# One of seven block products by 128-output matmuls, key sums and key rows by 32-output ones, and batch 2's rows loaded later, in a graph attention kernel

## The chip, the core and the metric

The kernel runs on one core of one Trainium2 chip. The metric is device time in microseconds (us) of one execution, as the median of several. A core has five engines that work side by side: TensorE (PE; its weight loads are shown as PEld), VectorE (DVE), ScalarE (ACT), GpSimd (POOL) and SyncE (SP), whose queue issues most DMAs here. TensorE multiplies a stationary operand (the loaded weights) with a moving one that streams by. All data is fp32.

## The reference

For each of 16 batches there are 512 rows `v` of 512 features, one conditioning row `q`, and an adjacency of 512 x 512 x 11 integers. Two attention directions attend from all 512 rows to the first 20 rows, with 16 heads of 32 features:

```python
row_zero = v.sum(-1) == 0
vcq = concatenate([v, where(row_zero[..., None], 0.0, q[:, None, :])], axis=-1)
self_feat = vcq @ W_self.T + b_self
output = self_feat
for d in range(2):
    A = adj if d == 0 else swapaxes(adj, 1, 2)
    A = A[:, :, :20, :]
    kv = self_feat[:, :20]
    aff = einsum(self_feat @ Wq[d].T + bq[d], kv @ Wk[d].T + bk[d]) / sqrt(32)
    aff = where(A.sum(-1) > 0, aff, -9e15) + A @ w_bias + b_bias
    w = softmax(aff)                       # over the 20 rows, for each head
    output += einsum(einsum(w, kv), Wout[d]) + bout[d]
return v + relu(output)
```

## The kernel before

**Setup (about the first 92 us).** Weights are loaded, and what depends on the first 20 rows of all batches at once (320 columns) is computed. The key sums (`kv_terms`, L532, tiles `ps_kv`) multiply 128 x 128 blocks of `W_self` with those rows: 16 matmuls with 128 outputs. The key rows (`key_rows`, L581, tiles `ps_k`) multiply `Wk`: eight calls of four 128-output matmuls, four calls ahead of the first burst of `keys` and one ahead of each of the next four bursts (L669, 32-row matmuls into `ps_g`). The `keys` bursts fold `Wq` and the keys into one matrix per batch, which goes to DRAM (`g_d`). Values (L644, `ps_v`) and batch 0's own features (`self_feat`, L202, `ps_sf`) lie between the bursts, in an order written out in `plan`. The row flags of batches 0 and 1 (L186, `ps_nz`) come from matmuls.

**The loop over 16 batches, four row tiles `nt` each.** All instructions are in a hand-written order (`manual_schedule`); each engine works through its own list in that order, SP's DMA queue too. While batch b is in its softmax stages, the features of batch b + 1 are made by a seven-product block scheme (`product`, L279; the sums of row blocks in `x_sum`, L244; sums joined in `partial` and `joined`): products 1 and 2 at `nt == 2`, products 6, 7 and 5 at `nt == 3`, products 4 and 3 at `nt == 0` of the next batch. Each product is two output halves times two input halves times four matmuls with 32 outputs and 246 columns, each four writing to the four 32-partition strips of one PSUM tile. Product 2 has a PSUM tile of its own, `ps_d`; the others share `ps_a` and `ps_c`.

Per row tile, `scores` (L353) makes 64 matmuls with 32 outputs and 152 columns into one of two `ps_s` tiles; `weigh` (DVE), `expo` (ACT), `normal` (DVE and POOL) and `turn` (DVE) make the softmax and its transpose. At `nt == 2` `attend` (L426, `ps_o`) applies the weights of the batch before to its values, with 32-row matmuls; `finish` and `residual` complete the output. At the very end the identity matmuls of `put_self` (L774) have 128 outputs.

A row whose sum is zero gets no `q`. For batches 2 and up, `load_xn` loads the batch's rows (two DMAs of 512 KB), `row_sum` (L166, four ACT instructions) sums them, `row_mask` (L170) turns the sums into flags on POOL and stores them by SP, and `load_nz` spreads them to all partitions for `partial`. For batch 2 the rows are loaded at batch 0, `nt == 1`, behind `load_adj(1, 1)`; their sums are made at batch 0, `nt == 3`, and the flags early in batch 1, `nt == 0`. `blocks` (L159) copies the values into block form by twelve DMAs at batch 0, `nt == 2`, after `clear_blocks` (L142) has filled the target with zeros; `load_values` (L136) reads it.

Of the kernel before, what the change touches and what calls it, by code (L numbers as in the profile page):

```python
# [13 lines left out]
P = 128  # L14
# [4 lines left out]
def gat_kernel(  # L19
# [20 lines left out]
    nc = tc.nc  # L40
    B, F, N = xT.shape
    NG, L = adj.shape[3], adj.shape[4]
    H, DH = 16, 32
    C = F // P
    HL = P // DH
    NT = N // P
    BM = B * NG
# [4 lines left out]
    R = P // HL  # L52
# [54 lines left out]
    def load_xn(b, h, ins=None):  # L107
        t = xns[b, h] = load.tile([P, 2, F], F32, tag="xn", name=f"xn{b}_{h}")
        behind(nc.sync.dma_start(t, xn[b].rearrange("(p j) f -> p j f", j=4)[:, 2 * h : 2 * h + 2]), ins)

    def load_adj(b, h, ins=None):
        t = adjs[b, h] = load.tile([P, 2, S * L], I32, tag="adj", name=f"adj{b}_{h}", bufs=3)
        a = adj[b, h * 2 * P : (h + 1) * 2 * P].rearrange("(t p) d m l -> p t (d m l)", p=P)
        behind(nc.sync.dma_start(t, a), ins)
# [131 lines left out]
    def product(b, n):  # L246

        w, x = {
            1: ((0, 0), lambda: x_block(b, 0, 0)),
            2: ((0, 1), lambda: x_block(b, 1, 0)),  # L250
            3: (3, lambda: x_block(b, 1, 1)),
            4: ((1, 1), lambda: sums[b, 4]),
            5: (0, lambda: sums[b, 1]),
            6: (1, lambda: sums[b, 2]),
            7: (2, lambda: sums[b, 3]),
        }[n]
        x = x()
        if n == 1:
            parts[b, "a"] = [bank(f"ps_a{b}_{i}", i) for i in range(2)]
        if n == 2:  # L260
            parts[b, "d"] = bank(f"ps_d{b}", 2)
        if n == 5:
            parts[b, "c"] = bank(f"ps_c{b}", 3)
        for i in range(2):
            for k in range(2):
                for a in range(HL):
                    at = i * P + a * R
                    if isinstance(w, tuple):
                        lhs = ws_v[:, 2 * w[1] + k, bass.ds(w[0] * F // 2 + at, R)]
                    else:  # L270
                        lhs = ws_s[:, w, k, bass.ds(at, R)]
                    if n in (2, 3, 5):
                        to = parts[b, "d" if n == 2 else "c"][bass.ts(a, R), bass.ts(i, HN)]
                        start = k == 0 if n == 2 else (n, i, k) == (5, 0, 0)
                        stop = k == 1 if n == 2 else (n, i, k) == (3, 1, 1)
                    else:
                        to = parts[b, "a"][i][bass.ts(a, R), :HN]
                        start, stop = (n, k) == (1, 0), (n, k) == (4, 1)
                    nc.tensor.matmul(to, lhs, x[:, k], start=start, stop=stop, skip_group_check=n != 2)  # L279
# [56 lines left out]
    def full_add(b, nt):  # L336
        f = fulls[b, nt] = msk.tile([P, H * S], F32, tag="full", name=f"full{b}_{nt}").rearrange(
            "p (g h m) -> p g h m", g=HL, m=S
        )
        shape = [P, HL, HL, S]  # L340
        nc.gpsimd.tensor_add(  # L341
            f, cqs[b].unsqueeze(1).to_broadcast(shape),
            adds[b, nt // 2][:, nt % 2].unsqueeze(2).to_broadcast(shape),
        )
# [108 lines left out]
    with tc.tile_pool(name="setup", bufs=1) as sp, tc.tile_pool(name="ps_acc", bufs=4, space=PSUM) as acc["pool"]:  # L453
# [18 lines left out]
        with tc.tile_pool(name="setup_k", bufs=1) as sk:  # L472
# [56 lines left out]
            kv_ps = [bank(f"ps_kv{fc}") for fc in range(C)]  # L529

            def kv_terms(fc, k):
                nc.tensor.matmul(  # L532
                    kv_ps[fc][:, :BM], ws_v[:, k, bass.ts(fc, P)], xkv[:, k],
                    start=(k == 0), stop=(k == C - 1),
                )

            for k in range(2):
                for fc in range(C):
# [38 lines left out]
            def key_rows(d, jc):  # L577

                ps = bank(f"ps_k{d}{jc}")
                for k in range(C):  # L580
                    nc.tensor.matmul(  # L581
                        ps[:, :BM], wk_sb[d][:, k, bass.ts(jc, P)], kvT[:, k],
                        start=(k == 0), stop=(k == C - 1),
                    )
                p3 = ps[:, :BM].rearrange("p (b m) -> p b m", m=NG)
                kh0 = msk.tile([P, B], F32, tag="kh0", name=f"kh0{d}{jc}", bufs=4)
                nc.scalar.activation(kh0, p3[:, :, 0], AF.Identity, bias=bk_sb[:, d, jc : jc + 1])
                nc.vector.scalar_tensor_tensor(
                    khD[:, d * C + jc].rearrange("p (b m) -> p b m", m=ND), p3[:, :, 1:],
                    bk_sb[:, d, jc : jc + 1], kh0.unsqueeze(2).to_broadcast([P, B, ND]),  # L590
                    ALU.add, ALU.subtract,
                )
# [176 lines left out]
    with tc.manual_schedule():  # L769
# [11 lines left out]
        for b in range(B):  # L781
# [7 lines left out]
            for nt in range(NT):  # L789
# [3 lines left out]
                if b == 0 and nt == 1:  # L793
                    load_adj(1, 0)
                    load_cq(1)
                    clear_blocks(zero)
                    load_adj(1, 1)
                    load_xn(2, 0)
                    load_xn(2, 1)
                if b == 0 and nt == 2:  # L800
                    blocks()
                if nt == 2 and last or nt == 3 and b == 0:
                    load_values(b)

# [7 lines left out]
                if nt == 0:  # L812
                    if b == 0:
                        for g in range(2):
                            scores(b, nt, g, ps[g])
                        mask_sum(b, 1)
                    else:
                        mask_mul(b, 1)
                        product(b, 4)
                        for g in range(2):  # L820
                            scores(b, nt, g, ps[g], range(2))
                        normal(*prev)
                        partial(b, 4, 1, 0, block(b, 1, 0))
                        if more:
                            load_x(b + 1, range(2), done["exp"])
                            load_x(b + 1, range(2, C), done["partial"])
                        for g in range(2):
                            scores(b, nt, g, ps[g], range(2, C))
                        if more:
                            row_mask(b + 1)  # L830
                        mask_count(b, 1)
                        joined(b, 3, "c", 1, 1)
                        product(b, 3)
                        mask_sum(b, 1)
                        if more:
                            load_adj(b + 1, 0, done["masks"])
                    mask_spread(b, 1, (0, 1))
                    if last:
                        biased = work.tile([P, C, N], F32, tag="o", name="biased")
                        for c in (2, 3):  # L840
                            nc.scalar.activation(biased[:, c], sfs[b][:, c], AF.Identity, bias=bo[:, c : c + 1])
                    s = weigh(b, nt, pair)
                    expo(s)
                    mask_spread(b, 1, (2, 3))
                    if prev is not None:
                        turn(*prev)
                    full_add(b, 1)
                    if more:
                        x_sum(b + 1, 1)
                    else:  # L850
                        for c in (2, 3):
                            nc.gpsimd.tensor_add(biased[:, c, N - P :], biased[:, c, N - P :], xs[b][:, c, N - P :])
# [60 lines left out]
                if nt == 3 and more:  # L913
                    mask_count(b + 1, 0)
                    product(b + 1, 6)
                    new_self(b + 1)
                    joined(b + 1, 1, "d", 0, 0)
                    x_sum(b + 1, 4)
                    if b + 2 < B:
                        for j in range(4):  # L920
                            row_sum(b + 2, j)
                    normal(*prev)
                    partial(b + 1, 2, 0, 1)
                    mask_sum(b + 1, 0)
                    if b > 0:
                        load_keys(b + 1, range(2, C), done["masks"])
                    mask_spread(b + 1, 0)
                    for g in range(2):
                        scores(b, nt, g, ps[g])
                    product(b + 1, 7)  # L930
                    product(b + 1, 5)
                    s = weigh(b, nt, pair, lambda: partial(b + 1, 3, 1, 1))
                    expo(s)
                    turn(*prev)
                    if b > 0:
                        residual(b - 1, 2, o)
                        store()
                        load_values(b)
                        residual(b - 1, 3, o)
                    full_add(b + 1, 0)  # L940
# [24 lines left out]
        b = B - 1  # L965
# [80 lines left out]
```

## Time and profile before

| | before |
|---|---|
| time, median of 3 | 592.53 us (591.71 to 592.59) |
| the profiled execution's own time | 593.27 us |
| its span | 591.5 us |
| TensorE busy | 578.7 us, 98% |
| weight loads busy | 439.7 us, 74% |
| VectorE, ScalarE, GpSimd busy | 492.3, 395.6, 384.2 us |
| granted TensorE clock | 0.995 of full |
| moved by DMA | 124.10 MB, 210 GB/s |

The page of the profile gives busy times for each engine. The chain of waits is followed back from the last instruction: its rows are start, duration, engine, output tile and line, and count. The order of time lists instructions by start, with the idle time ahead and what ended it in brackets; "issue" is time in which the engine waited for nothing that the profile shows. An fp32 matmul shows as two records, one per pass, each with a weight load of its own. A form such as `128*32 128x152` is the stationary operand's rows and outputs, and then the moving operand's rows and columns. Matmul ends are modelled, so this document measures from start to start.

### The profile page before, as it was taken

The page shows a single profiled execution, that of the slowest core. Times are in us where ns is not written, and L with a number is a line of the kernel's source. Part 1 is how long each engine was busy: PE and PEld are TensorE (multiplying, and loading weights), DVE is VectorE, ACT ScalarE, POOL GpSimd, SP SyncE. Part 2 cuts the span into 40 slices and gives each one's busy share as a digit, 9 for nine tenths or more (in the row PEclk, how much of TensorE's full clock was granted, in tenths as well). Part 3 has the DMA queues.
Part 4 walks back from the last instruction along what each step waited for, and adds up shares of the span by engine and source line. Part 5 has one row for each costly group of instructions (what it writes and reads, how often), then busy time and mean ns, then how long its engine had stood idle before and what let it go on. Part 6 is the DMA issues. An engine that isn't in the chain of part 4 may idle for free.

```text
span 591.5 us, 30038 instructions
## 1 busy us (share of the span) xinstructions
PE 578.7 (98%) x13180; PEld 439.7 (74%) x13180; DVE 492.3 (83%) x785; ACT 395.6 (67%) x1162; POOL 384.2 (65%) x351
## 2 busy tenths in 40 slices
PE   8999999999999999999999999999999999999994
PEld 6654547888978687787878787788787878787882
DVE  0495565889898888999999999888989898989896
ACT  1234644587877677768686868677787877777661
POOL 2315663638677675758686777675858677776774
PEclk9999999999999999999999999999999999999997
DMA  8998999857848485767676766757585748582503
GB/s 294 385 406 299 332 376 329 257 126 199 223 154 229 155 236 148 206 168 209 184 208 163 223 173 202 171 181 208 164 217 170 216 149 232 158 238 85 167 13 142
DMA packets 98129, 124.10 MB, mean 210 GB/s; under 512 B 19952, under 2 KB 70160, under 8 KB 95952
## 3 DMA queue, kind: packets, MB, share of 16 engines
q1 hardware_dynamic: 96752, 120.31, 67.1%
q8 instruction: 103, 1.69, 1.2%
q0 software_dynamic: 672, 1.36, 1.0%
q10 hardware_dynamic: 576, 0.53, 0.3%
q14 instruction: 26, 0.21, 0.1%
HBM read 82.30 MB, written 40.24 MB: 207 GB/s over the span
## 4 chain that ended last, share of the span: by engine, by line
PE 94%; DVE 3%; DMA 1%; issue 1%; ACT 0%; POOL 0%; SPq 0%; DVEq 0%; POOLq 0%; ACTq 0%
PE ps_s L353 44%; PE ps_a L279 17%; PE ps_c L279 8%; PE ps_o L426 6%; PE ps_d L279 4%; PE ps_v L644 3%; PE ps_k L581 3%; PE ps_sf L202 2%; DMA ws_q<-in_wsT 1%; PE ps_kv L532 1%; DVE o L435 0%; PE ps_nz L186 0%; DVE wt L415 0%; DVE ps_s L371 0%; DVE sm L406 0%
## 5 line engine op out<-in xcount | busy, mean ns | idle before, releaser
L353 PEld LDWEIGHTS ps_s<-g,sf 128*32 128x32 f32 x8192 | 264.0, 110 | 19.8 <-issue 12.2
L353 PE MATMUL ps_s<-g,sf 128*32 128x152 f32 x8192 | 277.3, 293 | 0.5 <-ACT st L684 0.5
L334 ACT COPY both<-add 32x80 f32<-32x80 f32 x512 | 130.9, 256 | 54.8 <-DVE add L325 49.0
L408 POOL TENSOR_TENSOR s<-s,sm 128x640 f32<-128x640 f32 x63 | 80.3, 1275 | 98.0 <-DVE sm L407 98.0
L341 POOL TENSOR_TENSOR full<-cq,both 128x640 f32<-128x640 f32 x64 | 100.1, 1565 | 30.3 <-issue 24.3
L314 ACT ACTIVATE prod<-adj,wb_sb 128x80 f32<-128x80 int32 x330 | 112.5, 432 | 0.0
L380 ACT ACTIVATE s<-s 128x640 f32<-128x640 f32 x63 | 46.5, 738 | 69.4 <-DVE s L375 69.0
L444 POOL TENSOR_TENSOR o<-o,x 128x512 f32<-128x512 f32 x60 | 75.9, 1285 | 0.0
L367 DVE TENSOR_TENSOR full<-ps_s,full 128x608 f32<-128x608 f32 x63 | 49.1, 779 | 32.1 <-PE ps_s L353 26.6
L406 DVE TENSOR_REDUCE sm<-s 128x32 f32<-128x640 f32 x63 | 50.9, 808 | 8.8 <-ACT s L380 8.6
L279 PE MATMUL ps_a<-t,ws_s 128*32 128x246 f32 x960 | 55.5, 370 | 0.0
L371 DVE TENSOR_REDUCE ps_s<-full 128x32 f32<-128x640 f32 x63 | 52.2, 828 | 2.2
L415 DVE STREAM_TRANSPOSE wt<-s 128x640 f32<-128x640 f32 x63 | 52.8, 839 | 0.1
L375 DVE TENSOR_TENSOR s<-full,ps_s 128x640 f32<-128x640 f32 x63 | 51.6, 818 | 1.1
L426 PE MATMUL ps_o<-wt,vd 32*32 32x512 f32 (+5 forms) x816 | 40.8, 581 | 3.7 <-DVE wt L400 2.0
L279 PEld LDWEIGHTS ps_a<-t,ws_s 128*32 128x32 f32 x960 | 32.2, 110 | 15.5
L325 DVE TENSOR_REDUCE add<-prod 128x80 f32<-128x960 f32 x32 | 36.8, 1150 | 6.3 <-ACT prod L314 4.4
L244 POOL TENSOR_TENSOR t<-x 128x492 f32<-128x492 f32 x30 | 34.4, 1148 | 10.1 <-DVE full L367 5.2
L439 ACT ACTIVATE o<-o,bo 128x512 f32<-128x512 f32 x60 | 38.2, 708 | 0.6 <-POOL biased L881 0.6
L435 DVE TENSOR_TENSOR o<-ps_o,sf 128x512 f32<-128x512 f32 x60 | 36.8, 672 | 1.0 <-PE ps_o L426 1.0
L286 DVE SCALAR_TENSOR_TENSOR u<-nz,qw,ps_a 128x246 f32<-128x246 f32 x90 | 36.6, 449 | 0.0
L244 POOL TENSOR_TENSOR t<-x,t 128x492 f32<-128x492 f32 x30 | 34.4, 1147 | 1.2
(238 smaller groups left out, 722.7 us busy)
## 6 DMA issues: line engine op xcount, KB each, us to landing
g_d<-st SPq DMA_DIRECT2D x16, 1064.0 KB, 5.9
g<-g_d SPq DMA_DIRECT2D x28, 608.0 KB, 5.2
out_T<-o SPq DMA_DIRECT2D x60, 256.0 KB, 4.7
xn<-in_xn SPq DMA_DIRECT2D x28, 512.0 KB, 3.6
x<-in_xT SPq DMA_DIRECT2D x28, 512.0 KB, 4.3
adj<-in_adj SPq DMA_DIRECT2D x32, 440.0 KB, 5.0
nz<-nz_d SPq DMA_DIRECT2D x14, 256.0 KB, 4.0
wk<-in_wkT SPq DMA_DIRECT2D x2, 1024.0 KB, 8.0
```

The costliest lines, as they stand in the source:

```text
L244: nc.gpsimd.tensor_sub(t, one, two)
L279: nc.tensor.matmul(to, lhs, x[:, k], start=start, stop=stop, skip_group_check=n != 2)
L314: nc.scalar.activation(p[:, :, l], a[:, :, l], AF.Identity, scale=wb_sb[:, l : l + 1])
L334: nc.scalar.copy(adds[b, h][bass.ts(a, R), :, g], add[r].rearrange("p (t m) -> p t m", t=2))
L341: nc.gpsimd.tensor_add(f, cqs[b].unsqueeze(1).to_broadcast(shape), adds[b, nt // 2][:, nt % 2].unsqueeze(2).to_broadcast(shape),)
L353: nc.tensor.matmul(bank[bass.ts(a, R), bass.ts(j, WD // HL)], sfs[b][:, k, bass.ds(nt * P + (2 * g + j) * R, R)], keys[:, k, a], start=(k ...
L371: nc.vector.tensor_reduce(mx, f, AX.X, ALU.max)
L375: nc.vector.tensor_sub(s, f, mx.unsqueeze(3).to_broadcast(full))
L408: done["normal"] = nc.gpsimd.tensor_mul(s, s, sm.unsqueeze(3).to_broadcast(full))
L415: nc.vector.transpose(wts[b][:, nt], s.rearrange("p a h m -> p (a h m)"))
L426: nc.tensor.matmul(banks[a][bass.ds(at // 2 * DH, n * DH)].rearrange("p (t n) -> p t n", n=32), vd[r, bass.ds(at * DH, n * DH)], wt[r, :, ...
L444: nc.gpsimd.tensor_add(o[:, c], o[:, c], xs[b][:, c])
```

## The change

Product 2 is made by 128-output matmuls: four instead of sixteen, on the same data into the same tile. The key sums and the key rows are made by 32-output matmuls instead, four for each one before, into the four strips of the same tiles. Per batch this leaves 1530 TensorE instructions. Batch 2's rows are loaded after `blocks` instead of before it; their sums move from batch 0, `nt == 3`, to batch 1, `nt == 0`, behind `mask_mul(1, 1)`, and their flags behind `full_add(1, 1)`, so that on SP their store comes after `load_adj(2, 0)`. For later batches the row sums stay where they are.

```diff
@@ product
-                for a in range(HL):
-                    at = i * P + a * R
+                wide = P if n == 2 else R
+                for a in range(P // wide):
+                    at = i * P + a * wide
                     if isinstance(w, tuple):
-                        lhs = ws_v[:, 2 * w[1] + k, bass.ds(w[0] * F // 2 + at, R)]
+                        lhs = ws_v[:, 2 * w[1] + k, bass.ds(w[0] * F // 2 + at, wide)]
                     else:
-                        lhs = ws_s[:, w, k, bass.ds(at, R)]
+                        lhs = ws_s[:, w, k, bass.ds(at, wide)]
                     if n in (2, 3, 5):
-                        to = parts[b, "d" if n == 2 else "c"][bass.ts(a, R), bass.ts(i, HN)]
+                        to = parts[b, "d" if n == 2 else "c"][bass.ts(a, wide), bass.ts(i, HN)]
...
@@ kv_terms
-                nc.tensor.matmul(
-                    kv_ps[fc][:, :BM], ws_v[:, k, bass.ts(fc, P)], xkv[:, k],
-                    start=(k == 0), stop=(k == C - 1),
-                )
+                for a in range(HL):
+                    nc.tensor.matmul(
+                        kv_ps[fc][bass.ts(a, R), :BM], ws_v[:, k, bass.ds(fc * P + a * R, R)], xkv[:, k],
+                        start=(k == 0), stop=(k == C - 1),
+                    )
@@ key_rows
-                    nc.tensor.matmul(
-                        ps[:, :BM], wk_sb[d][:, k, bass.ts(jc, P)], kvT[:, k],
-                        start=(k == 0), stop=(k == C - 1),
-                    )
+                    for a in range(HL):
+                        nc.tensor.matmul(
+                            ps[bass.ts(a, R), :BM], wk_sb[d][:, k, bass.ds(jc * P + a * R, R)], kvT[:, k],
+                            start=(k == 0), stop=(k == C - 1),
+                        )
@@ loop
                     load_adj(1, 1)
+                if b == 0 and nt == 2:
+                    blocks()
                     load_xn(2, 0)
                     load_xn(2, 1)
-                if b == 0 and nt == 2:
-                    blocks()
...
                         mask_mul(b, 1)
+                        if b == 1:
+                            for j in range(4):
+                                row_sum(2, j)
                         product(b, 4)
...
-                        if more:
+                        if more and b > 1:
                             row_mask(b + 1)
...
                     full_add(b, 1)
+                    if b == 1:
+                        row_mask(2)
...
-                    if b + 2 < B:
+                    if 0 < b < B - 2:
                         for j in range(4):
                             row_sum(b + 2, j)
```

## The prediction

> **What bounds the kernel now.** The page first: TensorE is busy all the time.
>
> ```profile
> PE 578.7 (98%) x13180; PEld 439.7 (74%) x13180; DVE 492.3 (83%) x785; ACT 395.6 (67%) x1162; POOL 384.2 (65%) x351
> ...
> q8 instruction: 103, 1.69, 1.2%
> ```
>
> TensorE (PE) and its weight loads (PEld) make 26,360 records, and queue q8, of kind "instruction", made 103 packets with 1.69 MB in all: 16.4 KB a packet, and 26,360/103 = 256 TensorE instructions a packet. So TensorE's own instructions come in blocks of 256. Next the chain of waits in order of time, rows of the attend stage (L426), which opens a batch's work once per batch:
>
> ```profile
> 133.59 2.17 PE ps_o L426 x48
> ...
> 195.02 1.04 PE ps_o L426 x25
> ...
> 226.92 0.98 PE ps_o L426 x4
> ...
> 258.97 2.17 PE ps_o L426 x48
> 289.44 2.17 PE ps_o L426 x48
> 319.92 2.17 PE ps_o L426 x48
> ...
> 381.08 1.05 PE ps_o L426 x27
> ...
> 413.08 2.84 PE ps_o L426 x48
> 444.22 2.17 PE ps_o L426 x48
> ...
> 535.83 2.17 PE ps_o L426 x48
> ```
>
> An undisturbed batch takes 30.48 us (289.44 to 319.92). The 13 batches from 133.59 to 535.83 take 402.24 instead of 13 x 30.48 = 396.24: 6.0 us are lost, nearly all in four batches, those from 195.02 (31.90), 226.92 (32.05), 381.08 (32.00) and 413.08 (31.14). What they lose stands in the order of time inside the attend stage, with the DMA view of the 0.9 us just before it (194.0 to 194.9):
>
> ```profile
> 194.95 1.11 PE L426 MATMUL ps_o<-wt,vd 32*32 32x512 f32 x25
> 196.45 1.06 PE L426 MATMUL ps_o<-wt,vd 32*32 32x512 f32 x7 [0.39 <-issue]
> ```
>
> ```profile
> q8 instruction: 1, 0.02, 6.8%
> ```
>
> TensorE stops in the middle of a run of like matmuls, waits for no engine ("issue"), and goes on about 1.5 us after an instruction packet. I read it as TensorE out of instructions: the block came late because its packet waited behind data. The lost batches come in a cycle: 195 and 227, then 381 and 413, six batches on. That is what blocks of 256 give if a batch has 1578 instructions = 6 x 256 + 42: the block boundaries move by 42 places a batch and are back after 256/42 = 6. 1578 is the change's own count of 1530 plus the 48 that it removes.
>
> **Product 2 by 128 outputs: what it adds.** Its records before:
>
> ```profile
> L279 PE MATMUL ps_d<-x,ws_v 128*32 128x246 f32 x480 | 27.9, 371 | 0.8 <-issue 0.8
> ```
>
> ```profile
> 141.51 1.88 PE L279 MATMUL ps_d<-x,ws_v 128*32 128x246 f32 x32
> 143.17 1.89 PE L279 MATMUL ps_a<-t,ws_s 128*32 128x246 f32 x32
> ```
>
> 480 over 15 batches is 32 passes for 16 matmuls: a matmul is two passes, with a load each. Start to start the product takes 1.66 us: eight groups of four side by side, 0.2075 us a group, 0.84 ns a column. A 128-wide pass runs at the same pace (eight passes of 320 columns in the row at 27.34 below take 2.35 us; less the 0.20 of a change of shape, worked out next, that is 0.27 each, 0.84 ns a column). So 8 wide passes replace 8 groups of narrow ones and in the stream nothing changes. What changes is the two switches of shape, into 128*128 and back:
>
> ```profile
> 576.57 0.31 PE L353 MATMUL ps_s<-g,sf 128*32 128x152 f32 x4
> 576.81 0.59 PE L774 MATMUL ps_o<-biased,ident 128*128 128x384 f32 x1
> 577.24 0.49 PE L774 MATMUL ps_o<-biased,ident 128*128 128x384 f32 x1
> ```
>
> ```profile
> 56.89 0.59 PE L186 MATMUL ps_nz<-rx,ones 128*128 128x512 f32 x1
> 57.41 0.41 PE L202 MATMUL ps_sf<-x,ws_v 128*32 128x236 f32 x4
> 57.63 0.38 PE L202 MATMUL ps_sf<-x,ws_v 128*32 128x236 f32 x4
> ```
>
> Into wide: 0.24 instead of 152 columns x 0.84 = 0.13, then 0.43 instead of 0.32: +0.22. Back: 0.52 instead of 0.43, then 0.22 instead of 0.20: +0.11. Together 0.33 a batch, on the engine that sets the end, with no cover: 15 x 0.33 = **+5.0**. The bounds are the same rows at 15 x 0.30 and 15 x 0.36 for the two-decimal reading.
>
> [...]
>
> **What it takes away: the late blocks.** 12 of 16 matmuls go, 48 instructions: 1530 = 6 x 256 - 6 a batch, so the block boundaries stand nearly still, 6 places a batch the other way. Where do they stand? The setup gains 48 + 96 matmuls (key sums 16 to 64, key rows 32 to 128), 576 instructions; the first product 2 loses 48; so at the first attend (133.59) the boundaries are moved by 528 = 2 x 256 + 16. Against batch 133.59's place that is +16, and in the last batches 16 - 14 x 6 = -68. In steps of 42 the batches of before stand at 0 (133.59), +42, +84 (195), +126 (227), then -88 (258.97), -46, -4 (319.92) and round again. The bad places are +84 and +126; all of +16 to -68 lies among -88, -46, -4 and the next place up, whose batches took 30.47 (258.97), 30.48 (289.44) and together 61.16 (319.92 to 381.08), and in the second round 91.61 for the three from 444.22 to 535.83. So I take away the **6.0** and leave **0.5** for the small losses of these seven (0.36 over 7 x 30.48, 0.05 each, times 15 is 0.8; none would be 0). Bounds: 4 to 6 removed, since a packet's delay varies with what data is queued.
>
> [...]
>
> **Key sums and key rows by 32 outputs.** One burst of key rows, 320 columns wide, in the chain of waits:
>
> ```profile
> 27.34 2.35 PE ps_k L581 x8
> ```
>
> The passes keep their pace; of 2.35 us some 0.20 is the open load after the switch in (the second step at 577.24, 0.43 for 0.32) and the switch out (0.52 for 0.43 at 57.41). A narrow pass opens with 0.02 instead (row 57.63), the switch out is alike: -0.08 for each of four later bursts, -0.3; the key sums gain a switch before the row-sum matmuls and lose one after the q product, taken as +0.1. Sum **-0.2**, between -0.6 and +0.2. The 576 extra instructions are fetched in a setup that uses the DMA heavily; at 64 instructions in 2.15 us a block lasts 8.6 us, against 4 to 5 in the loop, which covers that.
>
> **Batch 2's rows later.** The stop of the first batch, and the transfers before it:
>
> ```profile
> 110.06 0.60 PE L279 MATMUL ps_d<-x,ws_v 128*32 128x246 f32 x8
> 111.43 0.83 PE L279 MATMUL ps_d<-x,ws_v 128*32 128x246 f32 x12 [0.77 <-issue]
> ```
>
> ```profile
> 104.61 1.96 SPq L109 DMA_DIRECT2D xn<-in_xn  x2
> 109.83 12.07 SPq L159 DMA_DIRECT2D bd_d<-vw_d  x12
> ```
>
> From 110.06 to 111.43 is 1.37 for two groups of 0.2075: 0.96 lost, the same kind of stop. The 1 MB of rows queued at 104.61 is the last thing ahead of it; it moves behind the twelve block copies on SP's queue, to about 121. I count **-0.8** (0 to -0.96): another block may be late there. Passed on SP are only those copies and, behind the rows, the values' load, which waits for the copies to land anyway. On ScalarE the four row sums leave the first batch and come behind the next batch's eleven mask products:
>
> ```profile
> 112.91 0.62 ACT L166 ACTIVATE xn<-xn 128x512 f32<-128x512 f32 x1
> ...
> 122.61 3.76 ACT L314 ACTIVATE prod<-adj,wb_sb 128x80 f32<-128x80 int32 x11
> 127.65 2.13 ACT L334 COPY both<-add 32x80 f32<-32x80 f32 x8 [1.29 <-DVE add L325]
> ```
>
> 4 x 0.62 = 2.5 us go where ScalarE idled 1.29; the mask copies and the softmax behind them start some 1.2 later, once. TensorE works two score stages ahead of that softmax, so I count 0; if the rows land after 126.4, ScalarE's queue stands, and that is a rival. The row mask on GpSimd and its store on SP come some 1 to 4 us later, before a load whose user is over 5 us on: 0.
>
> **Sum.** The profiled execution took 593.27 (span 591.5 plus 1.77). 593.27 + 5.0 - 6.0 + 0.5 - 0.2 - 0.8 = 591.8, a change of -1.5; on the median 592.53, 0.74 below the profiled one, **591.0**. The ends of the terms (switches 4.5 to 5.4, blocks 6 to 4, small losses 0 to 0.8, setup -0.6 to +0.2, rows -0.96 to 0) add up to 589.5 and 594.9 for this case.
>
> **The rivals.** (1) The late blocks are not tied to the place in the batch, or the wait is one that the blocks only accompany: the 6.0 stays, the switches are paid, 592.53 + 5.0 - 0.2 less a part, 0.3, of the first batch's stop = 597.0. For it: single packets are late by chance, and 31.14 is only half a stop. Against: the six-batch cycle. It decides from half the stops on: with more than 3 us of them left the change is slower. 0.14. (2) My place is off by some 40 or more, and every batch has a stop of 0.7 to 1.5 us where two of six had one: 15 x 1.0 more than forecast, 606. 0.05. (3) Small losses of 0.2 (a batch more than these seven have on the whole: 61.16 is 0.2 over two) in every batch: 15 x 0.2 - 0.5, 593.5. 0.08. (4) The rows land late, ScalarE stands for them, and the delay passes by the softmax to VectorE and TensorE: 2 to 3 us once, 593.5. 0.07. (5) The wide loads lie open, eight times 0.10 (the first one's price at 576.81) less the one counted: 15 x 0.7 more, 601.5. 0.02. (6) The change does not do what it says: the instruction order has product 2 as four 128-output matmuls in all fifteen batches, so this gets nothing.
>
> **How the numbers follow.** The forecast's case has 0.64. About 0.2%, 1.2 us, is what can be told from no change, so faster means under 591.3. Of the forecast's 0.64 some 0.54 lies below that and 0.10 within it; (3) and (4) are within, or just beyond, 0.07 and 0.08; the rest is slower. Faster 0.54, same 0.17, slower 0.29. The range goes from 589.3 to 596.0: it takes in this case with its ends, (3), (4) and of (1) the part in which a sixth of the stops or more goes (0.04), and leaves out (2), (5) and the rest of (1), about 0.2 with a little below.
>
> **What would show it.** Right: product 2 as x8 with 0.33 more from start to start; attends evenly 30.8 apart in all batches, no "issue" gap inside one; key rows' bursts 0.08 shorter; no stop near 110. Wrong: attends 30.8 apart with further stops of about 1 us (rivals 1, 2), wide passes slower than 0.21 each (5), or a gap of the row sums on ScalarE near 126 followed by TensorE idle (4).

## The result and the profile after

The changed kernel took 593.49 us (median of 17 runs, 592.29 to 595.87), the kernel before on the same chip 591.71 (17 runs, 589.36 to 593.75): ratio 1.0039, 95% interval 1.0023 to 1.0055. It is slower by 0.4% where 1.5 us less (591.0 from 592.53) was forecast. The two profiled executions lie the other way round: 593.27 before, 592.87 after. Three later comparisons, in other runs on two chips, gave 0.9986 (0.9965 to 1.0008), 1.0021 (0.9999 to 1.0043) and 0.9994 (0.9980 to 1.0009), and the kernel before against itself 0.9997 (0.9980 to 1.0013). So only the first of four comparisons shows the change as slower, and none shows it as faster.

The page after. TensorE is as busy as before, in as many packets of instructions:

```profile
PE 578.8 (98%) x13108; PEld 434.4 (73%) x13108; DVE 491.8 (83%) x785; ACT 395.1 (67%) x1162; POOL 384.5 (65%) x351
...
q8 instruction: 103, 1.69, 1.1%
```

The chain of waits after, rows of the attend stage (now L427):

```profile
134.62 2.17 PE ps_o L427 x48
165.43 2.17 PE ps_o L427 x48
196.24 2.17 PE ps_o L427 x48
227.05 2.17 PE ps_o L427 x48
...
535.15 2.17 PE ps_o L427 x48
```

Each stage takes 2.17 us, none is broken up, and all 14 stand 30.81 apart (134.62 to 535.15 is 13 x 30.81): the 30.48 of an undisturbed batch before, and 0.33 for the two switches of shape. The groups of the attend stage's 32-output records, before and then after (records, busy us, mean ns, idle before them), say the same: 1.4 us of "issue" before, none after.

```profile
L426 PE MATMUL ps_o<-wt,vd 32*32 32x512 f32 x480 | 21.2, 599 | 1.4 <-issue 1.4
```

```profile
L427 PE MATMUL ps_o<-wt,vd 32*32 32x512 f32 x480 | 17.3, 599 | 0.0
```

So the loop did what was forecast. The first batch did not. The chain after, from the first scores on:

```profile
90.78 4.34 PE ps_s L354 x128
95.12 3.45 PE ps_sf L202 x64
98.57 4.39 PE ps_s L354 x136
102.96 0.31 issue
103.27 4.08 PE ps_s L354 x120
107.36 0.41 PE ps_a L280 x8
107.77 2.25 issue
110.02 1.45 PE ps_a L280 x24
```

The first scores begin 1.74 us earlier than before (92.52 there), but TensorE then stops twice in a run of like matmuls. Start to start, 0.49 us are lost at 102.65 and 2.46 at 107.35, 2.95 in all, where the kernel before lost 0.96 once. The DMA view of 102.4 to 107.4 has no instruction packet; that of 107.5 to 109.5 has the one that TensorE waits for:

```profile
q1 hardware_dynamic: 1731, 1.90, 106.0%
```

```profile
q8 instruction: 1, 0.02, 3.0%
```

In the first of the two stretches the data queue alone keeps all 16 DMA engines busy (106%). The packet's record begins at 107.58, and 2.4 us later TensorE goes on.

The kernel can be read in four pieces, from the first record of a stage to the first of the next: the setup up to the first scores; from there to the first attend stage; 13 batches; the rest with what lies around the span. In us, with the time of that execution, and the median and ratio of the timed runs:

| kernel | first scores | to attend | 13 batches | rest | profiled | median | ratio to before (95%) |
|---|---|---|---|---|---|---|---|
| before | 92.52 | 41.01 | 402.24 | 57.51 | 593.27 | 591.71 | |
| before, again (e13) | 91.88 | 40.92 | 402.18 | 58.62 | 593.60 | 593.23 | 0.9997 (0.9980-1.0013) |
| after | 90.78 | 43.77 | 400.53 | 57.79 | 592.87 | 593.49 | 1.0039 (1.0023-1.0055) |
| after, again (e9) | 92.31 | 42.47 | 400.54 | 57.79 | 593.11 | 593.79 | 0.9986 (0.9965-1.0008) |
| after, again (e15) | 91.63 | 44.68 | 400.66 | 57.77 | 594.74 | 594.75 | 1.0021 (0.9999-1.0043) |
| after, again (e18) | 91.53 | 42.77 | 400.53 | 57.77 | 592.60 | 593.02 | 0.9994 (0.9980-1.0009) |
| e1 product 2 only | 92.69 | 40.56 | 405.89 | 58.27 | 597.41 | 596.69 | 1.0069 (1.0051-1.0087) |
| e2 key sums, rows only | 91.08 | 42.10 | 399.45 | 59.13 | 591.76 | 593.38 | 1.0015 (1.0000-1.0030) |
| e3 later rows only | 92.70 | 42.03 | 401.92 | 58.01 | 594.66 | 594.00 | 1.0023 (1.0008-1.0038) |
| e6 after, rows early | 91.97 | 43.84 | 400.53 | 57.78 | 594.12 | 593.16 | 1.0044 (1.0028-1.0060) |
| e10 after, 128 more | 93.07 | 43.40 | 412.69 | 58.40 | 607.56 | 608.00 | 1.0228 (1.0201-1.0254) |
| e14 before, 128 more | 94.63 | 44.54 | 402.86 | 57.48 | 599.51 | 597.73 | 1.0085 (1.0063-1.0106) |
| e16 after, 192 more | 94.99 | 40.36 | 406.86 | 59.15 | 601.35 | 601.53 | 1.0139 (1.0118-1.0160) |
| e17 first batch moved | 90.82 | 41.34 | 401.19 | 57.78 | 591.13 | 592.09 | 0.9977 (0.9964-0.9990) |

Mean of four traces after less mean of two before: setup -0.6, to the first attend +2.5, 13 batches -1.6 (4.3 for switches, 5.9 of stops gone), rest -0.3: in sum, nothing.

### The profile page after: what moved, and what is told of

Read it like the earlier page. It is cut to its first block, busy times and chain, and to the rows that moved or that the text cites. A ratio compares the mean times of both kernels' runs of the same rounds, so it can differ in the third digit from the quotient of the medians.

```text
span 591.1 us, 29897 instructions
## 1 busy us (share of the span) xinstructions
PE 578.8 (98%) x13108; PEld 434.4 (73%) x13108; DVE 491.8 (83%) x785; ACT 395.1 (67%) x1162; POOL 384.5 (65%) x351
## 3 DMA queue, kind: packets, MB, share of 16 engines
q0 software_dynamic: 672, 1.36, 1.0%
## 4 chain that ended last, share of the span: by engine, by line
PE 95%; DVE 3%; issue 1%; ACT 0%; POOL 0%; DVEq 0%; POOLq 0%; ACTq 0%
PE ps_s L354 44%; PE ps_a L280 17%; PE ps_c L280 8%; PE ps_o L427 5%; PE ps_d L280 5%; PE ps_v L647 3%; PE ps_k L584 3%; PE ps_sf L202 2%; PE ps_kv L534 2%; PE ps_warm L492 1%; DVE o L436 0%; PE ps_nz L186 0%; DVE wt L416 0%; DVE ps_s L372 0%; DVE sm L407 0%
## 5 line engine op out<-in xcount | busy, mean ns | idle before, releaser
L280 PEld LDWEIGHTS ps_a<-t,ws_s 128*32 128x32 f32 x960 | 29.7, 110 | 18.8 <-POOL full L342 4.4
L427 PE MATMUL ps_o<-wt,vd 32*32 32x512 f32 (+5 forms) x816 | 36.4, 579 | 2.3 <-DVE wt L401 2.0
## 6 DMA issues: line engine op xcount, KB each, us to landing
g<-g_d SPq DMA_DIRECT2D x28, 608.0 KB, 4.9
```

Source lines behind the costliest of these rows:

```text
L427: nc.tensor.matmul(banks[a][bass.ds(at // 2 * DH, n * DH)].rearrange("p (t n) -> p t n", n=32), vd[r, bass.ds(at * DH, n * DH)], wt[r, :, ...
```

## The experiments

**The three parts, each alone in the kernel before.** Product 2 by 128 outputs only (e1):

> The kernel before with product 2 by 128 outputs and nothing else (the first part alone). Theory A (the switches of shape cost 0.335 us a batch and the blocks of 256 TensorE instructions come late only at some places of the batch, so 1530 instructions a batch take the late blocks away): +5.0 for 15 switches, less the four stops of the profiled execution before (6.0); the boundaries stand 48 instructions earlier than before at the first attend, -34 in the steps of the prediction, and reach -112 in the last batch, so no attend stops and batches take 30.81 us each. The stop of 0.96 us near 110 us stays, since nothing ahead of it has changed. Against the kernel before -1.0 to +0.6 us. Rival B (the late blocks come by chance, not by place): +5.0, stops inside attends remain. Rival C (the switch is dearer where it isn't profiled): +3 or more with no stop in the trace.

Measured: +4.3 us, 596.69 against 592.43. Neither A's number nor B's picture. Up to the ninth attend stage the batches take 30.81 us, but for two of 31.03 and 31.11; from there on every one is longer (chain of waits):

```profile
349.52 2.17 PE ps_o L427 x48
380.33 2.17 PE ps_o L427 x48
412.27 2.17 PE ps_o L427 x48
444.51 2.17 PE ps_o L427 x48
```

30.81, then 31.94 and 32.24, and so on to the end. The stops lie just ahead of the attend stage (410.6, 443.4, 475.0) and move into it (506.8), as boundaries that drift by six instructions a batch must. The pace of the switches is right and the place decides, but the bad stretch begins earlier than I had it, at about -88. Near 110 us at most 0.29 is lost instead of 0.96, with nothing changed ahead of it. Before, the stop came after eight records of product 2; here eight records are the whole product, so that TensorE wants the instruction behind them 1.86 us after the product's start (start to start in e16) instead of 0.42. A packet that is late by 0.96 at 0.42 is there by then.

Key sums and key rows by 32 outputs only (e2), and batch 2's rows later only (e3):

> The kernel before with the key sums and key rows by 32 outputs and nothing else (the second part alone). Theory A: the setup itself gains 1.2 to 1.5 us up to the first scores, but 576 more instructions move every later block boundary by 64 places; at 1578 a batch the batches then stand at 78, 120, 162, 204, 246, 32, 74, 116 and so on, of which about seven lie between 56 and 150, where four did: stops of about 1.5 us in some seven batches, and a stop of 2 to 3 us between 100 and 112 us in the place of the 0.96, because the block is asked for just as the zero fill of 2 MB is queued. In sum +2 to +5 us against the kernel before. Rival B (place does not matter): -1.5 to 0. The prediction's own term for this part was -0.2.

> The kernel before with batch 2's rows loaded after the block copies, their row sums in batch 1, and nothing else (the third part alone). Theory A: the block that is late at 110 us waits behind the zero fill of 2 MB and the adjacency load, not behind the rows; the instructions stand where they stood, so the stop of about 1 us stays and the time is that of the kernel before, -0.3 to +0.4. The prediction: -0.8, the stop near 110 gone. Rival U (the move itself is what made the changed kernel slower: row sums or row mask late, or the rows collide with the values' load): +1.5 to +3.

Measured: e2 +0.95 (0.0 to 1.8), e3 +1.6 (0.5 to 2.3). In e2 TensorE reaches the first scores earlier and loses 0.97 and 1.09 us at 103 and 108, as A says; but its batches lose only 3.2 us in 13 (399.45), not more than before, so the place of a single batch was misjudged again. In e3 the stop near 110 is still there (1.01 us) and another, 0.75, stands at 105.6: the prediction's -0.8 is refuted, A's zero too. Moving the rows costs something in the kernel before. The three single effects add up to +6.8 us, the whole change to +1.8 or less: the parts act on each other, and what the first two share is the place of the boundaries.

**Is it the zero fill?** SyncE's rows in the order of time, after:

```profile
93.94 0.37 SPq L130 DMA_DIRECT2D g<-g_d  x1
94.36 2.51 SPq L114 DMA_DIRECT2D adj<-in_adj  x1
96.91 2.31 SPq L119 DMA_DIRECT2D cq<-cq_d  x4
99.26 0.43 SPq L142 DMA_DIRECT2D bd_d<-zero  x1
99.73 3.16 SPq L114 DMA_DIRECT2D adj<-in_adj  x1
```

The 2 MB of zeros at 99.26 stood ahead of the late packets, so I took them for the cause. e4 issues them one step later, e5 in four parts during the setup:

```
e4  -  nt == 1: clear_blocks(zero)          e5  -  nt == 1: clear_blocks(zero)
    +  nt == 2: clear_blocks(zero)              +  setup, n in (4, 7, 10, 13):
       blocks()                                 +     clear_blocks(zero, quarter)
```

> The changed kernel with the zero fill of the block buffer issued just ahead of the block copies (step 2 of the first batch) and no longer ahead of the second adjacency load (step 1). Theory A: the two late blocks between 102 and 110 us (0.49 and 2.46 us lost) waited behind the fill; without it there they come in time, and a stop of at most 0.6 us is left in that stretch: 2 to 3 us less than the changed kernel, that is -1.2 to +0.2 against the kernel before. What can go wrong: the copies, and the values' load for the attend stage at 134 us, come some 6 us later, and that attend waits for them; then the gain is given back at 134. Rival U (the blocks were late because of the changed place of the rows, or of something else than the fill): the stop stays, +1.8 against the kernel before.

> The changed kernel with the zero fill of 2 MB cut into four parts and issued between the setup's stage stores (about 46, 57, 66 and 76 us), where a block of TensorE instructions lasts 8 to 10 us, and not at 99 us. The kernel with the fill one step later did not test this: SyncE runs ahead, and the fill was issued at the same time as before. Theory A (the blocks wanted at 102.7 and 107.4 us wait behind what is queued from 94 us on, of which the fill is half): they come in time, or some 0.5 us late; 2 to 3 us less than the changed kernel, so 590.5 to 591.5 with the kernel before at 591.7 to 592.4. What could spoil it: the stage stores leave little room, and TensorE waits for the setup's stage buffers, up to +3 us before 91 us. Rival D (the stop at 107 has nothing to do with the DMA load): the 2.46 us stay, 593.5.

Both missed: e4 594.40, +2.0 on the kernel before, e5 594.32, +3.6. e4 tested nothing: SyncE has no wait ahead of the fill and issued it at 100.56. e5 took the fill out of this stretch, and other loads moved into it. SyncE waited longer for the last stage stores, and the load of the key rows behind them went out at 98.12 instead of 93.94:

```profile
91.85 0.42 SPq L699 DMA_DIRECT2D g_d<-st  x1
98.12 0.37 SPq L130 DMA_DIRECT2D g<-g_d  x1
```

TensorE then stopped at 93.8 (1.36 us), 100.7 (0.38) and 105.2 (2.06). The DMA engines stay full until 107 or 108 us with the fill early or in its old place (e5: 1.01 busy from 106 to 108 us, 0.38 in the next 2; after: 0.96 from 104 to 108, 0.51 in the next 4); the fill alone was not the cause.

**Is it the rows, in the changed kernel?** e6 takes part three back.

> The changed kernel with batch 2's rows loaded, summed and masked where the kernel before did it (parts one and two of the change without part three). Theory A: the stops at 102 and 107 us stay near 3 us (their blocks wait behind loads that are queued before the rows); the loads at 118 to 131 us go, which alone cost +1.4 in the kernel before: 0.5 to 1.5 us less than the changed kernel. The prediction's term: 0.8 more than the changed kernel. Rival U (no effect in this place): within 0.4 of it.

593.16, +2.5 on the kernel before of that chip; 43.84 us from the first scores to the attend stage, within the 42.5 to 44.7 of the changed kernel. Rival U: in this place the rows make no difference that these runs can tell.

**Loads ahead of the attend stage.** In the kernel before, e7 issues the next batch's flags and bias rows after the stage; e8 does this and moves the fill as e5 does.

```
-  nt == 1: load_nz(b + 1, done["exp"]); load_cq(b + 1)
+  nt == 2, behind finish(): load_nz(b + 1, done["add"]); load_cq(b + 1)
```

> The kernel before, with the next batch's row flags (256 KB spread over 128 partitions) and bias rows (four loads) issued after the attend stage, behind the first addition of its result, and no longer 0.6 to 2.4 us ahead of the stage. Product 2, key sums and rows are those of before. Theory A (the blocks that are late in the attend stage are late because these loads are queued ahead of them when they are asked for, some 2.5 us before the stage): the blocks come 1 to 2 us earlier, the stops of the four bad batches (6.0 us in the profiled execution, some 4.5 on the median) go or shrink to under 0.4 each, and the time is 2.5 to 4.5 us less than before, without one switch of shape. Batches take 30.48 us. Rival E (the late block needs its 3 us whatever is queued): no change, 0 +- 0.5. Rival F (flags or bias rows now come too late for the partial sums): a wait on VectorE at about 9 us into the batch, slower.

> The kernel before with both moves: flags and bias rows after the attend stage, and the zero fill in four parts during the setup. Theory A: both kinds of stops go, the 0.96 us near 110 and those in the attend stages; 3 to 5.5 us less than the kernel before, 587 to 589. Rivals D and E: as for the two single moves.

e7: 592.01 against 590.68, +1.3 (0.4 to 2.0). The four bad batches took 30.91, 31.02, 31.58 and 31.73, so two lost 1.0 us less each and the last 0.6 more. The 13 batches of its trace take 400.60, 1.6 us less than in the traces of the kernel before, and yet the median is higher; 59.03 in the rest, where those have 57.51 and 58.62, is a part of that, and what else is not shown. e8: +3.0. Both missed their forecast. Moving loads shifted where TensorE starves (e5: to 93.8, 100.7 and 105.2 us); I found no order that ends it.

**The place of the boundaries, by itself.** The decisive runs change only the warm-up ahead of the first load: more and smaller products, so many instructions more, nothing else.

```
-  for _ in range(7):  matmul(warm[:, :P], ones, ones)
+  for _ in range(1):  matmul(warm[:, :P], ones, ones)
+  for _ in range(38): matmul(warm[:R, :4], ones[:, :R], ones[:, :4])      # e16: 54
```

> The changed kernel with other warm-up products ahead of the first load: one of 128 columns and 38 of 32 outputs and 4 columns in the place of seven of 128 columns, which adds 128 TensorE instructions ahead of all the work, so that every block boundary falls 128 instructions earlier in the work, and changes nothing else. Theory A (the place in the batch decides): in the steps of the prediction the batches stand at 158, 152, 146 and so on down to 80, nearly all in the bad stretch, so nearly every batch has a stop of 0.3 to 1.5 us at or just ahead of its attend stage: 6 to 14 us slower than the changed kernel, 599 to 607. Rival B (blocks late by chance, or where data is queued, whatever the place): 30.81 a batch as in the changed kernel, within 2 us of it.

> The kernel before with the warm-up products of the run that shifted the changed kernel by 128 instructions. Theory A: at 1578 instructions a batch the boundaries run through all places in six batches, so a shift only moves the stops to other batches (128 is about three steps of 42: the stops move by three batches, to the first and to the sixth and seventh of the thirteen, say): the time stays within 2 us of the kernel before, against the +14.2 us that the same shift cost the changed kernel. Rival H (the warm-up products themselves cost the 14 us, for instance by the clock or the first loads): +10 us or more here as well.

The shift of 128 made the changed kernel 14.2 us slower (608.0 against 593.79 for e9 on the same chip). Its batches take 30.91 to 32.67 us where all took 30.81, and in its chain of waits the attend stages are drawn out (over 2.17) or begin behind a stop (fewer than x48):

```profile
136.54 2.17 PE ps_o L427 x48
168.03 2.27 PE ps_o L427 x48
...
231.61 3.15 PE ps_o L427 x48
264.62 2.18 PE ps_o L427 x41
295.44 2.36 PE ps_o L427 x48
327.72 2.15 PE ps_o L427 x35
358.51 2.89 PE ps_o L427 x48
```

13 batches grew by 12.2 us. The same shift in the kernel before (e14) left them at 402.86, +0.7 on e13, and only moved the stops to other batches, 1, 5, 6, 7, 11 and 13:

```profile
139.24 3.23 PE ps_o L426 x48
170.77 2.17 PE ps_o L426 x48
...
294.06 3.06 PE ps_o L426 x48
325.45 3.23 PE ps_o L426 x48
357.08 2.17 PE ps_o L426 x48
```

Rival H fails: the batches did not slow down. The kernel still lost 4.5 us (597.73 against 593.23 for e13), more than the 2 I allowed: in the traces 2.7 up to the first scores (1.5 of it is the longer warm-up: the first key sums start at 5.91 instead of 4.46), and 3.6 to the first attend stage, where one stop is now 2.8 us. That was the hint for the last question.

> The kernel before once more, with a trace from another execution and perhaps another chip. Theory A (the loss that the change removes is the stops of the bad places, whose size goes with the delay of each packet): the same batches stop, third, fourth, ninth and tenth of the thirteen, the others take 30.48 us; the stops of the 13 batches add up to less than the 6.0 us of the first trace where the time is lower (4.4 us where the median is 591.7), and to more where it is higher (7 us at 594.5). If other batches stop, the place doesn't decide in this kernel.

> The changed kernel once more, on the chip of the three beside it. Theory A (loop without stops, so that from the first attend stage on it takes a fixed 458.3 us, and all that varies lies ahead of that stage): 14 batches of 30.81 us in the trace, stops of 2.5 to 4 us between 92 and 112 us, 1 to 2.5 us slower than the kernel before. If batches in the middle of the run stop in the trace this time, the place of the block boundaries does not decide.

> The changed kernel beside the kernel before on this chip. Theory A: its 14 batches take 30.81 us each again, its time is 458.3 us plus the start of the first attend stage, 593 to 594 on any chip; the ratio to the kernel before follows from the kernel before alone: above 1.002 where that has its median under 592.3, about 1 where it has 593.5 or more.

e13 has its stops in the same four batches as the first trace (chain of waits):

```profile
195.84 2.10 PE ps_o L426 x23
226.25 3.26 PE ps_o L426 x48
...
381.68 2.10 PE ps_o L426 x21
413.13 2.19 PE ps_o L426 x42
```

The loop of the changed kernel is the same in four traces to 0.13 us (one batch of 30.94 in e15). e15 missed by 0.75 us; its trace has the longest stretch between the first scores and the attend stage, 44.68.

**The place in the first batch.** The 576 instructions added to the setup move the boundaries by 64 in the stretch from 91 to 134 us too. e16 moves them back there with 192 instructions more in the warm-up (256 less 64).

> The changed kernel with warm-up products that add 192 instructions (one of 128 columns and 54 of 32 outputs and 4 columns in the place of seven of 128). 192 is 256 less 64, so in the first batch the boundaries fall where the kernel before has them. The longer warm-up puts all the work some 1 to 2 us later, so what counts is the stretch from the first scores to the first attend stage: 41.0 us in the two traces of the kernel before, 43.8, 42.5 and 44.7 in those of the changed kernel. Theory A (the place of the boundaries makes the stops at the start): 41.0 plus 0.3 for the switch plus at most 0.5, so 41.3 to 41.9; and in the run the batches go from place -34 to -118 as with the wide product alone, so the last five or so stop by 0.3 to 1.4 each: 3 to 6 us more than the changed kernel in all, with the warm-up. Rival U (rows, narrow key sums or the loads make the stops, whatever the place): 43 to 44.5 us.

```profile
94.99 4.34 PE L354 MATMUL ps_s<-g,sf 128*32 128x152 f32 x128 [0.52 <-ACT st L689]
99.14 3.64 PE L202 MATMUL ps_sf<-x,ws_v 128*32 128x256 f32 x64
102.60 8.45 PE L354 MATMUL ps_s<-g,sf 128*32 128x152 f32 x256
110.86 1.84 PE L280 MATMUL ps_a<-x,ws_v 128*32 128x246 f32 x32
```

In the order of time of e16 all 256 score passes and the product behind them run through without an "issue". The stretch took 40.36 us, less than A's 41.3 to 41.9 and far from the rival's 43 to 44.5. That all the work starts later is not the reason: e14 reaches the first scores as late (94.63) and has its stop of 2.8 us. The late batches stop as in e1, the first of the 13 took 32.01, which A does not have, and with the warm-up the kernel took 601.53, 8.5 more than e18 where I said 3 to 6.

e17 moves the boundaries back by 48, in the first batch only, and e18 is the changed kernel beside it:

```
-  wide = P if n == 2 else R              # product
+  wide = P if n == 2 and b > 1 else R
   # key rows: (d, jc) == (1, 3) by 128 outputs again, the other seven by 32
```

> The changed kernel with the last key-row product of the first weights (second quarter from the end of the eight) by 128 outputs again, 48 instructions fewer in the setup, and batch 1's product 2 by 32 outputs, 48 instructions more behind the first batch's scores: the boundaries of the first batch move 48 places back towards those of the kernel before, and those of all later batches stay where the changed kernel has them. Theory A: the stretch from the first scores to the first attend stage 41.2 to 42.5 us instead of 42.5 to 44.7, batches of 30.81 us without stops: 1 to 2.5 us less than the changed kernel. Rival U: the same stops at the start, 0.3 less for one switch fewer.

> The changed kernel beside the two on the same chip: 14 batches of 30.81 us, 42.5 to 44.7 us from the first scores to the first attend stage, 593 to 595 in all.

e17 took 592.09: ratio 0.9977 (0.9964 to 0.9990) to the kernel before on that chip, and 0.93 us less than e18, a little under the 1 to 2.5 of A. The two intervals overlap (e18: 0.9980 to 1.0009), so the times alone do not settle it; the traces say more. The stop at the end of the first product, 2.46 us in the changed kernel's first trace and 2.38 in e18, is 1.29 start to start (chain of waits of e17); one batch of 31.47 is the only other loss:

```profile
98.61 8.27 PE ps_s L354 x256
106.88 1.66 PE ps_a L280 x32
108.54 1.10 issue
109.64 1.87 PE ps_d L280 x32
```

**The place, counted.** TensorE's instructions can be counted in a trace: matmul records, weight loads and its waits for semaphores, in the order of their starts, from the first of the program on. From one attend stage to the next they are 1578 in the kernel before and 1530 in the changed one, as the prediction has it. From the first scores on, the 20 traces hold 61 idle times of TensorE of more than 0.1 us that the profile calls "issue". Counted on in 256s, every one of them ends at place 194 or 195, whatever the kernel, the shift and the order of the loads, and every one ends 2.2 to 2.6 us after the start of an instruction packet's record. The chains shown here have it too: before, the stop comes after eight records of product 2; in the changed kernel after eight of product 1, 32 records or 64 instructions earlier; in e17 after all 32 of product 1, 48 instructions later than that.

So the stops are TensorE waiting for a block, and an edit chooses which work stands at the boundary. Why one packet is late and the next is not stays argued. In the 4 us ahead of a stop the data keep the DMA engines 0.74 to 1.10 busy in the first batch, but 0.29 to 0.96 in the later ones (0.50, 0.58 and 0.61 ahead of 196.06, 227.90 and 382.13 before), so full engines are not needed for it, and none of the runs that move loads isolates a cause.

**An order that failed.** e11 and e12 put the fill first and load batch 1's keys only behind the block copies.

```
-  load_keys(1)  (ahead of the loop)      +  clear_blocks(zero)
   nt == 2: blocks()                      +  load_keys(1)
```

> The changed kernel with the loads at the start of the loop in another order: the zero fill is issued first (at about 92 us), and batch 1's key rows (1.2 MB), whose user is at 137 us, only after the block copies, about 111 us. So 1.2 MB less is queued between 94 and 108 us, where the late blocks are asked for. Theory A (a block waits for what is queued when it is asked for): the stops between 92 and 112 us, 2.95 us in the changed kernel's profiled execution, shrink to 0.5 to 1.5: 1.5 to 2.5 us less than the changed kernel. Theory G (the packet's wait goes with the DMA engines being saturated at all, not with how much stands ahead): the stops stay above 2.5 us, no gain.

> The kernel before with the key sums and key rows by 32 outputs (which alone took 0.9 us more) and the loads at the start of the loop in the order of the run before this one. Theory A: the setup's gain of 1.3 us is kept and the stops at the start (2.06 us with the narrow key sums alone) shrink to about 0.5 to 1: 1 to 2 us less than the narrow setup alone, so 0 to 1 us less than the kernel before. Theory G: as the narrow setup alone, +0.9.

e11: 593.15, ratio 0.9973 (0.9959 to 0.9987) to a kernel before that took 594.49 there, 0.6 less than e9, which these runs do not tell from nothing, and not A's 1.5 to 2.5; the stop at 107 went, others of 1.24, 0.51 and 0.43 came. e12 was 3.6 us slower than before: the scores of batch 1's keys came too soon for the load (order of time):

```profile
128.42 6.01 PE L353 MATMUL ps_s<-g,sf 128*32 128x152 f32 x128 [2.12 <-DMA g<-g_d]
```

## Why the prediction was wrong

*What bounds the kernel* and *the switches of shape, +5.0*: right. 30.81 less 30.48 is 0.33, in every batch of four traces but the one of 30.94. The wide passes did not slow down: after, the first three of a product start at 142.65, 142.96 and 143.17, so 0.31 apart once and then 0.21, the pace of the groups of four before (0.2075). So the fifth rival, an estimate that had every wide load lie open at the price of the first, is out.

*The late blocks, -6.0*: right in that the place of the boundaries makes the stops and, against the traces, in size: 13 batches took 400.53 instead of 402.24 plus 4.3. That the packet waited behind data, or that its delay varies with what is queued (the bound of 4), no run shows. TensorE goes on 2.45 us after the start of the packet's record at 196.45, not about 1.5. And a part is luck: the prediction took -88 for a good place, e1 has its first long batch there, and the changed kernel's last batch, at -68, is three batches short of it. One block boundary cost 2.46 us in the trace after (at 107.35). The first rival (not tied to the place) fell with e10 and e14. The second, boundaries in a bad place in every batch, was priced at 606: e10 put them there and took 608.0. *Small losses, +0.5*: none; 30.81 holds to 0.01 in the first trace.

*Batch 2's rows later, -0.8* is the first step that failed. It took the rows for what stood ahead of the late packet at 110, because they were the last thing queued. With the rows gone from there the stop stayed in e3 (1.01 us) and grew in the changed kernel to 2.95. The fourth rival, ScalarE, is not the reason: after, TensorE loses 0.4 us in all from 111.47 to the attend stage, in the scores from 129.86 on, and in e9, e15 and e18 nothing in those scores.

*Key sums and key rows, -0.2* is the second. Its own work gained more than that, 0.6 in the mean of the traces (the two of the kernel before differ by as much). But its 576 instructions move every boundary behind them, which I worked out for the loop and not for the stretch ahead of it: there I only asked whether a block lasts long enough in the setup. The shift costs 2.5 us from 91 us to the attend stage, less 0.33 for a switch, as e16 and e17 show by taking it back. With the measured terms the sum is 5.0 - 6.0 + 0 - 0.6 + 2.1 = +0.5 instead of -1.5, and the rest is 0.6 shorter (0.3 on balance, with one of the 15 switches in it): about nothing. The 593.49 measured lies within the forecast's range, but not by the third or fourth rival, which would have put it there.

*From the trace to the median*: the forecast took all of 6.0 off a median that lay 0.74 below the profiled execution, as if what differs between executions had nothing to do with the stops. Over the groups of runs the medians of the kernel before went from 590.68 to 594.49; those of the changed kernel, in four groups, from 593.02 to 594.75. In these four groups the change loses where the kernel before is quickest, and does not where it is slowest. That the kernel before has smaller stops in its 590 us executions would explain it, but both of its traces come from executions of over 593; it stays open, and so does the rest of the 1.8 us on the first chip.

## What to carry to other kernels

Where an engine's instructions come in blocks, as TensorE's do here (26,360 records in 103 packets before, 256 a packet), an edit that changes their number moves every later boundary: work out where the boundaries fall in each stretch of the program, not in the loop alone (64 places cost some 2.1 us in the first batch here), and test it by adding idle instructions ahead of everything (128 cost 14.2 us here). Taking out the transfer that was last in the queue did not take away the stop behind it (1.01 us in e3, 0.96 before): do not put a late packet down to one transfer without a run that moves that transfer alone. And such a loss should be sized over several executions, for the profiled one may not be typical (593.27 before, where the median of 17 is 591.71).

## What the runs showed that I had not expected

128 instructions in a warm-up, which do no work, cost 14.2 us of 594; the same 128 in a kernel with 48 more instructions a batch left its 13 batches within 0.7 us of what they took. From the start of the packet's record to TensorE's next matmul are 2.4 us (107.58 to 110.02), of which the packet's record takes about 1 us (3.0% of 16 engines in 2 us), and it is 2.2 to 2.6 at all 61 stops. The kernel before differs by 3.8 us of median between groups of runs (590.68 and 594.49), more than any edit tried here but the shifts and product 2 alone; only comparisons within a group could be read.
